# Attention's projections and the shares' transposition in the array's column halves, placed next to the values' product

## The chip, the cores and the metric

The kernel runs on one core of a Trainium2 chip. The time is the device time of one execution in microseconds (us); the kernel before took 5586.81 us (median of 3 runs, 5586.36 to 5594.37). Beside it stands one execution that the hardware profiler took, and all durations come from that one.

## The reference

The input is two images of 256 channels and 64x64 pixels, in fp32. Four layers follow each other:

```python
xn = group_norm(x)
q, k, v = split(einsum('bchw,oc->bohw', xn, w_qkv), 4 heads of 64 channels)
attn = softmax(einsum('bhci,bhcj->bhij', q, k) * 64 ** -0.5)
x = xn + einsum('bchw,oc->bohw', attn @ v, w_proj) + b_proj      # layer 0
x = x + position term                                            # layer 1
x = relu(x + bottleneck with one deformable 3x3 convolution)     # layer 2
x = x + two deformable 3x3 convolutions with group norms         # layer 3
```

The change is in layer 0: 4096 pixels attend to 4096 pixels, in 4 heads, for each of the two images.

## The kernel before, in words

The function `attention` (from L148 on) does layer 0 and, woven into it, much of layer 2; `deform` does what is left of layer 2 and layer 3 after it.

**Tiling of the attention.** A unit (`units`, L213) is one image and one pair of heads, so there are four. A unit has 256 steps (`per_unit`, L353). A step n takes 128 pixels of q, one head (h) and one of four chunks of 1024 keys (c), and a block is the 16 steps of 256 pixels of q. Each step runs through four functions:

- `scores` (L526) multiplies q by k (L533): contraction over the 64 channels of a head, so two products go side by side in the two row halves of the 128x128 array; the profile writes that as 64\*128 (64 rows by 128 columns). VectorE (DVE) takes the negated row maximum (`low`, L542).
- `exponentials` (L545) applies exp on ScalarE (ACT) with that maximum as bias (L549).
- `turn` (L555) transposes the exponentials with 16 matmuls of 64\*128 (L561) into two PSUM tiles `tt`; `keep` (L568) copies these to SBUF, one by ACT (L578) and the other by DVE (L576); from unit 2 on both go to ACT for h = 1.
- `attend` (L580) multiplies by the values (L588): contraction over 128 keys, 64 channels of output for each head, so two heads go side by side in the two column halves, written 128\*64.

All fp32 products but the transpositions stand in the profile as two matmul instructions each.

**Order of the work.** The engines run in the order in which the program is written (`manual_schedule`). The main loop takes two steps per turn. TensorE (PE) sees: the scores of steps n + 2 and n + 3; `small(n)`; `turn(n)`; the values' product of n - 4 and n - 3; `small(n + 1)`; `turn(n + 1)`; in units 2 and 3, a background step. On ACT the order is: copy of n - 1, `small(n)`, exp(n + 2), copy of n, `small(n + 1)`, exp(n + 3). On DVE: copy of n - 1, both maxima, `small(n)`, copy of n, the output of `attend`, `small(n + 1)`.

**What `small` runs.** `small(at)` (L635) runs what was registered for step `at` by `due` (L357), and where nothing was, in units 2 and 3, a background step of layer 2 (`background`, L606). Registered are:

- `make_q` (L243): the projection to q for the next 512 pixels, at even steps: 128\*128, two products of 512 columns (L247), then ACT scales it and a DMA turns the halves round. 31 of them stand in the main loop.
- `keys` (L257, matmuls L262), 24 of them: they use the column halves before the change already. One of two is at an odd step and one at an even one.
- `values` (L270, matmuls L275), 24: eight products of 128 columns, 128\*128; one of two at an odd step and one at an even one.
- For each block, `compare`, `raised`, `weights`, `spread`, `combine`: they turn the maxima and sums of the four chunks into shares. `spread` (L457), at an even step, transposes the 128x16 tile `share` (L460), DVE copies the result (L462), and DMAs write it to DRAM and read it back widened (`f`). `combine` multiplies the output of `attend` by it on POOL (L474 to L482), four steps later.
- For each pair of blocks, `project(0)` at an odd and `project(1)` at an even step (L493, matmul L498): 128\*128, one product of 512 columns each, then a DVE operation adds it to the residual `res`.
- In units 1 and 3, `second_layer` (L514) at an even step: layer 2's first product (L840, 128\*64) and its ACT operations.

All of these and the background steps write one PSUM tile, `pm`, which has one buffer (`pms`, L168); each waits until the one before it has been read by ACT or DVE.

Work in `begin` (L305), before the main loop, uses `make_q`, `keys` and `values` too.

Of the kernel before, what the change touches and what calls it, by code (L numbers as in the profile page):

```python
# [9 lines left out]
F32 = mybir.dt.float32  # L10
# [8 lines left out]
P = 128  # L19
# [19 lines left out]
class Net:  # L39
# [108 lines left out]
    def attention(self, bott):  # L148
# [4 lines left out]
        tc, nc, a = self.tc, self.nc, self.a  # L153
        with ExitStack() as ctx:
            wp = ctx.enter_context(tc.tile_pool(name="att_w", bufs=1))
            work = ctx.enter_context(tc.tile_pool(name="att_work", bufs=2))
            one = ctx.enter_context(tc.tile_pool(name="att_one", bufs=1))
# [18 lines left out]
            def ps(shape):  # L176
                return pms.tile(shape, F32, name="pm")

            def rows(t):
                return t.rearrange("(cb p) n -> p cb n", p=P)  # L180
# [8 lines left out]
            halves = [slice(0, 64), slice(64, 128)]  # L189
# [7 lines left out]
            for i in range(NB):  # L197
                t = xp.tile([P, 2, 512], F32, name="xb") if i < 4 else rest[:, i - 4]
                nc.sync.dma_start(t, rows(a["x"][0])[:, :, 512 * i : 512 * i + 512])
                first.append(t)  # L200
                if i == 1:
                    for j in range(2):
                        at = slice(64 * j, 64 * j + 5)
                        nc.sync.dma_start(wpos[at], a["wpos"])
                        nc.sync.dma_start(pos[at], a["pos"][:, :, P * j : P * j + P])
            wqkv = wp.tile([P, 2, 3 * C], F32, name="wqkv")
# [3 lines left out]
            wproj = wp.tile([P, 2, C], F32, name="wproj")  # L210
# [25 lines left out]
            def prepare(b):  # L236
                for coef in stats_of(b, (block(a["x"][b], i) for i in range(NB))):
                    yield True
                for i in range(NB):
                    normalize(b, i, coef, block(a["x"][b], i))  # L240
                    yield True

            def make_q(u, i, x, dst):  # L243

                hp = units[u][1]
                for cb in range(2):
                    nc.tensor.matmul(  # L247
                        dst, lhsT=wqkv[:, cb, hp * P : hp * P + P], rhs=x[:, cb, :],
                        start=(cb == 0), stop=(cb == 1),
                    )  # L250
                t, s = (qp.tile([P, 512], F32, name=n) for n in ("q", "qs"))
                nc.scalar.mul(t, dst, 64**-0.5)
                for j in range(2):
                    nc.sync.dma_start(s[halves[j], :], t[halves[1 - j], :])
                q[u, i] = (t, s)
# [14 lines left out]
            def values(u, x, dst):  # L270

                at = 2 * C + units[u][1] * P
                for n in range(4):
                    for cb in range(2):
                        nc.tensor.matmul(  # L275
                            dst[:, n * P : (n + 1) * P],
                            lhsT=x[:, cb, n * P : (n + 1) * P],
                            rhs=wqkv[:, cb, at : at + P],
                            start=(cb == 0),
                            stop=(cb == 1),  # L280
                        )

            def tiles(t):
                return t.rearrange("p (t c) -> p t c", c=P)
# [119 lines left out]
            class Block:  # L404
# [36 lines left out]
                def weights(self):  # L441

                    w = self.w
                    nc.vector.tensor_mul(self.sum, self.sum, w)
                    total = one.tile([P, 4], F32, name="total")
                    nc.vector.tensor_reduce(total, self.sum, AX.X, ALU.add)
                    nc.vector.reciprocal(total, total)
                    self.share = work.tile([P, 2, 4, 2], F32, name="share")
                    nc.vector.tensor_mul(
                        self.share.rearrange("p h c t -> p t h c"),  # L450
                        w.rearrange("p (t h) c -> p t h c", h=2),
                        total.rearrange("p (t h) -> p t h", h=2).unsqueeze(3).to_broadcast(
                            [P, 2, 2, 4]
                        ),
                    )

                def spread(self):  # L457

                    pt = ps([P, 512])[:16, :P]
                    nc.tensor.transpose(pt, self.share.rearrange("p h c t -> p (h c t)"), self.ident)  # L460
                    t = one.tile([16, P], F32, name="shares")
                    nc.vector.tensor_copy(t, pt)  # L462
                    d = self.share_d[self.i % 2]
                    nc.sync.dma_start(d, t)
                    self.f = one.tile([P, 4, 256], F32, name="f")
                    for h in range(2):
                        src = d[8 * h : 8 * h + 8].rearrange("(c t) q -> c (t q)", t=2)
                        nc.sync.dma_start(
                            self.f[halves[h]], src.unsqueeze(0).to_broadcast([64, 4, 256])
                        )  # L470
# [22 lines left out]
                def project(self, ob):  # L493
                    b, hp = units[self.u]
                    i = self.i // 2
                    oc = slice(ob * P, ob * P + P)
                    pp = ps([P, 512])
                    nc.tensor.matmul(  # L498
                        pp, lhsT=wproj[:, hp, oc], rhs=self.av, start=True, stop=True
                    )  # L500
                    res = self.res[:, ob, :]
                    if hp == 0:
                        nc.vector.scalar_tensor_tensor(
                            res, pp, self.vec[:, V_BPROJ + ob : V_BPROJ + ob + 1], res,
                            ALU.add, ALU.add,
                        )
                    else:
                        nc.vector.tensor_add(res, res, pp)
                    if ob == 1:
                        nc.sync.dma_start(  # L510
                            rows(self.xa_d[b])[:, :, 512 * i : 512 * i + 512], self.res
                        )
# [9 lines left out]
            def parts(n):  # L522
                u, r = divmod(n, per_unit)
                return u, r // 16, r % 16 // 4, r % 4 // 2, r % 2
# [43 lines left out]
            def keep(n, pts):  # L568
                u, i, c, t, h = parts(n)
                if n % 4 == 0:  # L570
                    ets[n // 4] = etp.tile([P, 8, 2, 256], F32, name="et")
                for j, pt in enumerate(pts):
                    at = P * t + 64 * j
                    dst = ets[n // 4][:, :, h, at : at + 64]
                    if j and (u < 2 or h == 0):
                        nc.vector.tensor_copy(dst, pt)  # L576
                    else:
                        nc.scalar.copy(dst, pt)  # L578
# [20 lines left out]
            def first_batch():  # L599
                yield from bott.conv(0, bt, ps)  # L600
                yield from self.early_image(bott, bt, ps)

            ets, now = {}, {}
            back = []

# [10 lines left out]


            pts, e = {}, {}
            ready = self.small.tile([P, 1], F32, name="ready")
            begin()  # L620
            n = 0
            while n < last + 4 or back or any(own.values()):
                u, d = divmod(n, per_unit)
                if d == 0 and u < len(units):
                    plan_unit(u)
                    if u == 0:
                        back.append(prepare(1))
                    if u == 1:
                        back.append(bott.before(0, bt, ps))
                    if u == 2:  # L630
                        back.append(first_batch())
                    if u == 3:
                        back.insert(0, bott.before(1, bt, ps))

                def small(at):  # L635
                    steps = own.pop(at, ())
                    for f in steps:
                        f()
                    if not steps and u > 1:
                        background(1)  # L640

                if n - 1 in pts:
                    keep(n - 1, pts.pop(n - 1))
                ahead = [(m, scores(m)) for m in (n + 2, n + 3) if m < last]
                small(n)
                for m in range(2):
                    if n < last:
                        pts[n + m] = turn(e.pop(n + m))
                    if ahead:
                        at, sc = ahead.pop(0)  # L650
                        e[at] = exponentials(at, sc)
                    if m == 0:
                        if n < last:
                            keep(n, pts.pop(n))
                        if 4 <= n < last + 4:
                            attend(n - 4)
                            attend(n - 3)
                        small(n + 1)
                if u or n % 8 == 0:
                    background(1)  # L660
                n += 2
# [813 lines left out]
```

## Time and profile before

| what | us |
|---|---|
| median of 3 runs | 5586.81 |
| the profiled execution's own time | 5402.33 |
| its span, first to last instruction | 5400.6 |
| from 0 to 75: start, positions, first q, k and v | 75 |
| from 75 to 1440: units 0 and 1, PE busy | 1351.92 of 1365 |
| from 1440 to 3140: units 2 and 3 with layer 2, PE busy | 1594.95 of 1700 |
| from 3140 to 5400: deformable convolutions, PE busy | 1972.77 of 2260 |

The time of an execution in the profiler is 3.3% under the median of the runs without it. A matmul's bar begins when the product starts to stream and is longer than the distance to the next one, since matmuls are pipelined: what a group costs PE is read from the start of its first matmul to the start of the next group's first. A group in the timeline (x16) is merged from so many instructions; the number after the start is its length. A name after the arrow in brackets says what ended an idle time.

### The profile page before, as it was taken

Reading aid. Unit: us, or ns where it says so; the run is one execution under the profiler, and the core shown is the slowest. Engines: PE = TensorE matmul, PEld = TensorE weight load, DVE = VectorE, ACT = ScalarE, POOL = GpSimd, SP = SyncE. Lnnn points to the kernel's source line nnn. Section 1 sums busy time; section 2 is a strip of 40 time slices with the busy share of each in tenths; the row PEclk is TensorE's granted clock in tenths of the full one; section 3 lists DMA queues with packets and bytes.
Section 4 is the critical chain, followed back from the end, with each engine's and each line's share of the span. In section 5 each row is a group of like instructions: output and inputs, shape, how many; then the busy total and the mean of one; then the engine's idle time right before and its main releaser. Section 6 shows DMA issues by size and latency. Waiting matters only on the chain.

```text
span 5400.6 us, 97530 instructions
## 1 busy us (share of the span) xinstructions
PE 4976.3 (92%) x37208; PEld 2665.3 (49%) x37208; DVE 4249.0 (79%) x8066; ACT 2897.7 (54%) x5333; POOL 2068.6 (38%) x1946
## 2 busy tenths in 40 slices
PE   8999999999999999999999977767899999999998
PEld 5555555555555555555555533333444444444443
DVE  6877767787668888677766648787899999999998
ACT  5676656666566666566666622222444444444444
POOL 0111101000024343233200047777566566656665
PEclk9999999999999999999999978888999999999999
DMA  5221111101113222222141146666999999999998
GB/s 168 62 89 58 41 64 39 48 29 44 48 54 89 77 82 90 80 78 74 50 136 34 35 156 231 225 223 231 353 333 330 341 360 358 352 390 353 342 349 320
DMA packets 347363, 920.29 MB, mean 170 GB/s; under 512 B 58972, under 2 KB 98698, under 8 KB 346894
## 3 DMA queue, kind: packets, MB, share of 16 engines
q0 software_dynamic: 193536, 679.59, 35.4%
q1 hardware_dynamic: 153358, 234.46, 13.5%
q8 instruction: 292, 4.78, 0.4%
q14 instruction: 177, 1.45, 0.1%
HBM read 815.90 MB, written 89.60 MB: 168 GB/s over the span
## 4 chain that ended last, share of the span: by engine, by line
PE 65%; DVE 17%; issue 6%; DMA 5%; ACT 5%; POOL 2%; SPq 0%; ACTq 0%; DVEq 0%; POOLq 0%
PE sc L533 14%; PE av L588 14%; PE out L1276 10%; PE tt L561 9%; DVE smp L1245 8%; PE pd L726 5%; DMA four<-img,didx 3%; PE pt L1257 3%; DVE low L542 2%; ACT e L549 2%; PE pm L976 1%; POOL bfour L766 1%; DVE bfour L947 1%; PE pm L498 1%; PE pm L247 1%
## 5 line engine op out<-in xcount | busy, mean ns | idle before, releaser
L1245 DVE SCALAR_TENSOR_TENSOR smp<-four,dw,smp 128x256 f32<-128x256 f32 x3456 | 1611.8, 483 | 168.5 <-ACT smp L1239 85.5
L549 ACT ACTIVATE e<-sc,low 128x1024 f32<-128x1024 f32 x1024 | 1147.5, 1121 | 646.0 <-DVE low L542 645.0
L542 DVE TENSOR_REDUCE low<-sc 128x1 f32<-128x1024 f32 x1024 | 1209.5, 1219 | 295.9 <-PE sc L533 288.2
L766 POOL DMA_INDIRECT four<-img,didx x1152 | 1161.5, 1008 | 656.8 <-DVE smp L1245 307.7
L1276 PE MATMUL out<-st,wc 128*128 128x512 f32 x2304 | 1236.8, 619 | 139.7 <-ACT st L1266 111.3
L533 PE MATMUL sc<-k,qs 64*128 64x512 f32 x2048 | 1029.0, 621 | 7.4 <-ACT e L549 7.1
L533 PE MATMUL sc<-k,q 64*128 64x512 f32 x2048 | 1018.7, 620 | 0.0
L588 PE MATMUL av<-et,v 128*64 128x256 f32 x8192 | 999.1, 386 | 0.0
L561 PEld LDWEIGHTS tt<-ident,e 64*128 64x128 f32 x16384 | 647.9, 140 | 559.1 <-issue 245.0
L474 POOL TENSOR_TENSOR o<-o,f 128x1024 f32<-128x1024 f32 x64 | 153.4, 2396 | 1967.1 <-DVE o L428 1182.8
L766 POOL DMA_INDIRECT bfour<-img,bidx x576 | 579.8, 1007 | 665.6 <-DVE bsmp L957 487.3
L561 PE MATMUL tt<-ident,e 64*128 64x64 f32 x16384 | 751.2, 228 | 86.5 <-ACT et L578 69.4
L578 ACT COPY et<-tt 128x512 f32<-128x512 f32 x1280 | 722.2, 587 | 83.7 <-PE tt L561 80.6
L1239 ACT ACTIVATE smp<-four,dw 128x256 f32<-128x256 f32 x1152 | 524.2, 503 | 430.6 <-DMA four<-img,didx 368.9
L576 DVE COPY et<-tt 128x512 f32<-128x512 f32 x768 | 524.6, 683 | 247.3 <-PE tt L561 245.8
L1257 PEld LDWEIGHTS pt<-ident,smp 128*128 128x128 f32 x2304 | 321.1, 144 | 740.7 <-issue 439.1
L1266 ACT COPY st<-pt 128x1024 f32<-128x1024 f32 x288 | 291.0, 1010 | 721.2 <-PE pt L1257 721.2
L588 PEld LDWEIGHTS av<-et,v 128*64 128x64 f32 x8192 | 544.8, 137 | 257.0 <-issue 1.3
L1276 PEld LDWEIGHTS out<-st,wc 128*128 128x128 f32 x2304 | 393.3, 197 | 402.2 <-issue 207.1
L1257 PE MATMUL pt<-ident,smp 128*128 128x128 f32 x2304 | 457.7, 281 | 67.0 <-DVE smp L1245 61.7
L726 PE MATMUL pd<-x,wf 128*126 128x512 f32 (+2 forms) x896 | 460.8, 601 | 8.4 <-DVE wf L1131 7.3
L533 PEld LDWEIGHTS sc<-k,qs 64*128 64x128 f32 x2048 | 351.2, 192 | 229.7 <-issue 123.6
(153 smaller groups left out, 3369.1 us busy)
## 6 DMA issues: line engine op xcount, KB each, us to landing
f<-share_d SPq DMA_DIRECT2D x128, 256.0 KB, 3.9
xb<-xn SPq DMA_DIRECT2D x55, 512.0 KB, 4.0
img<-imgt SPq DMA_DIRECT2D x96, 256.0 KB, 7.0
four<-img,didx POOLq DMA_INDIRECT x1152, 6.1
xa<-res SPq DMA_DIRECT2D x32, 512.0 KB, 2.7
xb<-in_x SPq DMA_DIRECT2D x20, 512.0 KB, 5.4
bfour<-img,bidx POOLq DMA_INDIRECT x576, 3.0
qs<-q SPq DMA_DIRECT2D x64, 128.0 KB, 4.0
```

The costliest lines, as they stand in the source:

```text
L533: nc.tensor.matmul(s[:, j, :], lhsT=q[u, i // 2][int(h != j)][halves[j], at : at + P], rhs=k[u][c][halves[j], h, :], start=True, stop=True,)
L542: nc.vector.tensor_reduce(low, s, AX.X, ALU.max, negate=True)
L549: nc.scalar.activation(e.rearrange("p j n -> p (j n)"), s, AF.Exp, bias=blk.low[:, g, c : c + 1], accum_out=blk.sum[:, g, c : c + 1],)
L561: nc.tensor.transpose(pt[:, m, :], e[half, m // 4, m % 4 * P : m % 4 * P + P], self.ident[half, half],)
L576: nc.vector.tensor_copy(dst, pt)
L578: nc.scalar.copy(dst, pt)
L588: nc.tensor.matmul(now["av"][halves[h], :], lhsT=v[u][c][:, m, halves[h]], rhs=ets[j][:, m, h, :], start=(m == 0), stop=(m == 7),)
L726: nc.tensor.matmul(pd[:m, r0 * W : r1 * W], lhsT=wt(s, t), rhs=src[:, (y + r0) * W : (y + r1) * W], start=(n == 0), stop=(n == len(srcs) * ...
L766: self.nc.gpsimd.indirect_dma_start(out=dst, out_offset=None, in_=img, in_offset=bass.IndirectOffsetOnAxis(ap=idx, axis=0),)
L1245: nc.vector.scalar_tensor_tensor(smps[s], four[:, c], weight(s, c), smps[s], ALU.mult, ALU.add)
L1257: nc.tensor.transpose(pts[u][:, c, j * P : (j + 1) * P], smp[:, c * P : c * P + P], self.ident,)
L1276: nc.tensor.matmul(outs[ob], lhsT=wc[k][:, c, ob * P : ob * P + P], rhs=sts[u][:, c, :], start=(k == 0 and c == 0), stop=(k == K2 - 1 and ...
```

## The change

Four edits inside `attention`:

1. `make_q`, `values` and `project` split each product into two with 64 columns of weights (pixels or output channels), which write partitions 0 to 63 and 64 to 127 of the same PSUM tile from the same moving operand. There are twice as many matmuls and weight loads, each with half of the columns.
2. `share` becomes one tile of 128x64, made and zeroed by POOL once before the main loop, in which `weights` fills the first 16 columns. `spread` transposes all 64, into 64 partitions, and copies 16 of these.
3. `small(n)` moves from between the scores and `turn(n)` to after `keep(n)`, right ahead of `attend(n - 4)`. PE then sees: scores, scores, `turn(n)`, `small(n)`, values' product, `small(n + 1)`, `turn(n + 1)`. On ACT `small(n)` comes after exp(n + 2) and the copy of n; on DVE after the copy of n. Background steps that run in `small(n)` move with it.
4. `ready`, a scratch column that is written once at the start, takes a buffer of another scratch tile.

```diff
@@ make_q
-                    nc.tensor.matmul(
-                        dst, lhsT=wqkv[:, cb, hp * P : hp * P + P], rhs=x[:, cb, :],
-                        start=(cb == 0), stop=(cb == 1),
-                    )
+                    for j in range(2):
+                        at = hp * P + 64 * j
+                        nc.tensor.matmul(
+                            dst[halves[j]], lhsT=wqkv[:, cb, at : at + 64], rhs=x[:, cb, :],
+                            start=(cb == 0), stop=(cb == 1),
+                        )
@@ values
-                        nc.tensor.matmul(
-                            dst[:, n * P : (n + 1) * P],
-                            lhsT=x[:, cb, n * P : (n + 1) * P],
...
+                        for j in range(2):
+                            px = n * P + 64 * j
+                            nc.tensor.matmul(
+                                dst[halves[j], n * P : (n + 1) * P],
+                                lhsT=x[:, cb, px : px + 64],
...
@@ weights
-                    self.share = work.tile([P, 2, 4, 2], F32, name="share")
                     nc.vector.tensor_mul(
-                        self.share.rearrange("p h c t -> p t h c"),
+                        share[:, :16].rearrange("p (h c t) -> p t h c", h=2, c=4),
@@ spread
-                    pt = ps([P, 512])[:16, :P]
-                    nc.tensor.transpose(pt, self.share.rearrange("p h c t -> p (h c t)"), self.ident)
+                    pt = ps([P, 512])[:64, :P]
+                    nc.tensor.transpose(pt, share, self.ident)
                     t = one.tile([16, P], F32, name="shares")
-                    nc.vector.tensor_copy(t, pt)
+                    nc.vector.tensor_copy(t, pt[:16])
@@ project
-                    nc.tensor.matmul(
-                        pp, lhsT=wproj[:, hp, oc], rhs=self.av, start=True, stop=True
-                    )
+                    for j in range(2):
+                        at = ob * P + 64 * j
+                        nc.tensor.matmul(
+                            pp[halves[j]], lhsT=wproj[:, hp, at : at + 64], rhs=self.av,
+                            start=True, stop=True,
+                        )
@@ attention, before and in the main loop
+            share = one.tile([P, 64], F32, name="share")
+            nc.gpsimd.memset(share, 0.0)
...
-            ready = self.small.tile([P, 1], F32, name="ready")
+            ready = self.small.tile([P, 4], F32, name="rs_t")[:, :1]
...
                 ahead = [(m, scores(m)) for m in (n + 2, n + 3) if m < last]
-                small(n)
                 for m in range(2):
                     if n < last:
                         pts[n + m] = turn(e.pop(n + m))
...
                     if m == 0:
                         if n < last:
                             keep(n, pts.pop(n))
+
+                        small(n)
                         if 4 <= n < last + 4:
                             attend(n - 4)
                             attend(n - 3)
```

More of the change, by code (lines that the diff above doesn't have):

```diff
@@ L274, in values @@
                     for cb in range(2):
-                        nc.tensor.matmul(
-                            dst[:, n * P : (n + 1) * P],
-                            lhsT=x[:, cb, n * P : (n + 1) * P],
-                            rhs=wqkv[:, cb, at : at + P],
-                            start=(cb == 0),
-                            stop=(cb == 1),
-                        )
+                        for j in range(2):
[3 more added lines that the diff above has]
+                                lhsT=x[:, cb, px : px + 64],
+                                rhs=wqkv[:, cb, at : at + P],
+                                start=(cb == 0),
+                                stop=(cb == 1),
+                            )
             def tiles(t):
@@ L495, in project @@
                     i = self.i // 2
-                    oc = slice(ob * P, ob * P + P)
                     pp = ps([P, 512])
-                    nc.tensor.matmul(
-                        pp, lhsT=wproj[:, hp, oc], rhs=self.av, start=True, stop=True
-                    )
+                    for j in range(2):
[3 more added lines that the diff above has]
+                            start=True, stop=True,
+                        )
                     res = self.res[:, ob, :]
```

## The prediction

> **What bounds the kernel now.** I read the busy time by stage first, to see where the edited code runs and which engine is full there.
>
> ```profile
> 75.00:1440.00 1365.00, 1351.92 (x14451) 779.07 (x14447) 1033.72 (x1499) 876.44 (x1621) 151.78 (x100) 1.00 0.17 52
> 1440.00:3140.00 1700.00, 1594.95 (x15697) 915.17 (x15697) 1219.08 (x1885) 1087.92 (x2022) 451.01 (x395) 0.97 0.24 72
> ```
>
> The columns are the stretch, its length, busy PE, weight loads, DVE, ACT and POOL (instructions in brackets), granted clock, DMA share and GB/s. All edited code runs in these two stretches and in the 75 us before them. In the first PE is busy 99%, in the second 94%; DVE has 76% and 72%, ACT 64% both times. PE sets the pace, alone in the first and nearly so in the second. After 3140 nothing is edited, so what attention saves should pass to the end as it is.
>
> Second, the waits of PE, for the second stretch: what it does when it isn't the bound.
>
> ```profile
> PE tt L561 <- ACT et L578: 60.7, 38, 3.4
> PE tt L561 <- DVE et L576: 14.9, 32, 1.6
> PE pm L904 <- ACT bod L895: 11.5, 7, 1.6
> ```
>
> (us in total, times, longest.) The first stretch has 5.3 us of the first kind and 1.0 of the second. So `turn` sometimes waits until `keep` has emptied its PSUM tile, and layer 2's background steps are what makes that late.
>
> Third, the timeline of PE, to price each step from start to start.
>
> ```profile
> 721.04 1.95 PE L588 MATMUL av<-et,v 128*64 128x256 f32 x16
> 722.82 1.89 PE L262 MATMUL pm<-xb,wqkv 128*64 128x512 f32 x8
> 724.63 0.71 PE L561 MATMUL tt<-ident,e 64*128 64x64 f32 x16
> ...
> 731.95 2.05 PE L275 MATMUL pm<-wqkv,xb 128*128 128x128 f32 x16
> 733.93 0.71 PE L561 MATMUL tt<-ident,e 64*128 64x64 f32 x16
> ...
> 776.81 0.66 PE L561 MATMUL tt<-ident,e 64*128 64x64 f32 x16
> 777.40 1.95 PE L588 MATMUL av<-et,v 128*64 128x256 f32 x16
> 779.28 0.71 PE L561 MATMUL tt<-ident,e 64*128 64x64 f32 x16
> 779.83 0.65 PE L533 MATMUL sc<-k,q 64*128 64x512 f32 x1
> ...
> 781.60 0.66 PE L561 MATMUL tt<-ident,e 64*128 64x64 f32 x16
> ...
> 788.86 1.13 PE L498 MATMUL pm<-avs,wproj 128*128 128x512 f32 x2
> 789.91 0.71 PE L561 MATMUL tt<-ident,e 64*128 64x64 f32 x16
> ...
> 801.25 0.65 PE L533 MATMUL sc<-k,q 64*128 64x512 f32 x1
> ...
> 803.11 0.28 PE L460 MATMUL pm<-ident,share 128*16 128x128 f32 x1
> 803.32 0.72 PE L561 MATMUL tt<-ident,e 64*128 64x64 f32 x16
> 803.97 1.95 PE L588 MATMUL av<-et,v 128*64 128x256 f32 x16
> ...
> 808.26 1.98 PE L247 MATMUL pm<-xb,wqkv 128*128 128x512 f32 x4
> 810.17 0.71 PE L561 MATMUL tt<-ident,e 64*128 64x64 f32 x16
> ```
>
> A plain turn of the loop is 4.79 us (776.81 to 781.60): transposes 0.59, values' product 1.88, transposes 0.55, scores 1.77. Watch the overlaps at the seams: the product with the values ends at 779.35 and the transposes start at 779.28, 0.07 earlier; where the form stays (64\*128 to 64\*128) the same seam overlaps by 0.16. The keys (L262) follow the product in its own form, and the two take 3.59 us together (721.04 to 724.63), only 1.71 more than the product alone. A seam between forms costs about 0.1 us.
>
> **What the Trainium skill says.** "TensorEngine Tiling (Array Packing)", Key Properties: "Changing tiling mode (not just tile) drains the TensorE". The trace agrees, at the 0.09 us above. Its Restrictions say that column tiling disables the transpose mode for fp32; but the shares' transposition is 128\*16 already and takes 277 ns, and layer 2's transposes take 297 ns as 128\*64 (L967) and 296 as 128\*128, so the trace shows no price. "TensorE: Matmul & The Clock Gate", Part 2, says that weight loads are pulled ahead of running matmuls and cost by columns; the trace has loads of 87 ns for 16 columns, 137 for 64 and 186 to 190 for 128, and no matmul waits for them. "PSUM — Partial Sum Buffer", on bank collisions, has it that different column tiles may write one bank at the same time; the keys do that in `pm` today.
>
> **The change part by part.** A step at an even place stands before between scores and transposes. It costs its own length, 0.09 for the seam after the scores and 0.06 for transposes that start cold: at 801.25 the scores take 1.86 to L460 instead of 1.77, and the transposes then take 0.65 instead of 0.59. So 0.15 plus its length. A step at an odd place follows the product and has one seam in its length. Afterwards both stand beside the product in its form, and cost their streaming alone: the keys' 1.71 for four pairs of 512 columns, 0.43 a pair. That halves run side by side is what the keys show; there each half has a moving operand of its own, in the new products both have the same.
>
> - `make_q`, 31 in the loop, even: 1.91 + 0.15 = 2.06 before; four pairs, 1.71 after. 31 x 0.35 = 10.9 us.
> - `project(1)`, even, 31: 1.05 + 0.15 = 1.20 before; two pairs, 0.86 after. 31 x 0.34 = 10.5 us.
> - `project(0)`, odd, 31: 1.05 against 0.86. 31 x 0.19 = 5.9 us.
> - Keys at even places, 12: 1.86 + 0.15 = 2.01 against 1.71. 3.6 us. The odd ones stay as they are.
> - Values: 16 instructions of 281 ns take 2.05, so one each (2.05 - 0.28) / 15 = 0.118. Sixteen pairs after: 1.89, if pairs keep that pitch. Twelve even ones, 1.98 + 0.15 = 2.13 before: 2.9 us; twelve odd ones, 1.98: 1.1 us. The unknown is the loads: 32 of 64 columns instead of 16 of 128. The product with the values has half of its 0.223 a pair as the lower bound, 0.11, or 1.8 us; if each load of 137 ns stood alone, 4.4 us, or 60 us lost over all 24. I take 0.118, since the transposes load 128 columns into each of two halves every 0.07 us.
> - Shares, 63 beside scores: 0.21 + 0.15 = 0.36 before; one product of 128 columns, 0.12 after. The load of 64 columns instead of 16 is hidden as others are. 63 x 0.24 = 15.1 us. The memset and the 48 zero columns cost PE nothing, and DVE the same copy of 16 rows.
> - Layer 2's first product (L840), 15 even: 1.86 + 0.15 against 1.71. 4.5 us. Background steps in `small(n)`: 13 groups of full-array transposes lose one of two seams, 0.15 each, and two groups of 128\*64 0.3: 2.6 us.
> - `begin` (a few seams) and `ready`: under 1 us, not counted.
>
> Sum: 10.9 + 10.5 + 5.9 + 3.6 + 2.9 + 1.1 + 15.1 + 4.5 + 2.6 = **57 us**, half of it in each stretch.
>
> **What the move delays.** On ACT the step's copy now stands ahead of exp(n + 3) and no longer ahead of exp(n + 2). For `make_q`: from the start of the scores, PE ends q at 1.77 + 0.59 + 1.71 = 4.1; ACT copies until 4.9, exp ends at 6.1. The scores that need that PSUM tile start at 4.1 + 1.88 + 0.55 + 0.86 = 7.4: 1.3 us of cover. The single buffer of `pm` is now read while only the product (1.88) runs, before transposes too: ACT's 4.9 or DVE's copy after `keep` at about 4.8 against 6.0 for the odd step. Where keys and shares fall on one step (3 times), PE waits about 0.8 as it does today. Odd values and keys still delay exp, and the scores after them wait 0.5 as now. The shares' DMAs (SP) and `f` come about 0.7 us later, after `keep`'s copy on DVE; POOL's `combine` waits for them or for the output of `attend`, and is done over 3 us before DVE writes that buffer again; its gathers behind it lose at most those 0.7. In the second stretch DVE's copy in `keep` no longer stands behind `small(n)`, which takes from the 14.9 us; but two background steps now stand ahead of exp(n + 3), which can give it back. I count it at nothing, between 15 gained and 15 lost.
>
> The profiled execution would go from 5402.33 to 5345, 1.1% less. The median is 184 us above it, for reasons that the profile doesn't show; I subtract the same 57 there: 5587 - 57 = **5530 us**.
>
> **The rivals.**
> - *Second half absorbed.* If units 2 and 3 follow the chain scores, maximum, exp, `keep` and not PE, only the first stretch's half counts: 28 us, 5558. For it: that chain leaves under 0.1 us in a plain turn there (ACT's copy starts at 1501.71 and takes 0.58, and the transposes start at 1502.40). Against: the steps lie in turns that are longer on PE.
> - *The halves don't run side by side when they share the moving operand.* Then q costs 1.71 more, a projection 0.86, values 1.89: 31 x 1.71 + 62 x 0.86 + 24 x 1.89 = 152 us, less 57: 95 slower, 5682. It decides from 38% lost overlap on. Against: keys and the values' product overlap fully, with other operands.
> - *Waits shrink too*, by more than 15 us: 5510.
>
> **How the numbers follow.** Main case 5530 (5512 to 5546): 0.66. Half absorbed, 5546 to 5575: 0.17. More gained, 5500 to 5512: 0.07. About no change: 0.04. Slower: 0.06. Range 5508 to 5562. Faster 0.9, within 0.2% 0.04, slower 0.06; 0.2%, 11 us, is about what a measurement of this kernel can tell.
>
> **What would show it.** q as eight instructions of 128\*64 in about 1.8 us, projections as four in about 1.0, values as 32 in about 2.0, each right before or after the values' product; scores 1.77 to the transposes in nearly all turns; PE's waits in the second stretch within 15 us of before. Bars twice as long for q would show serial halves; more waits of `tt` for `et` absorption.

## The result, and the profile after

| kernel | median us | lowest to highest | runs |
|---|---|---|---|
| before | 5586.59 | 5586.31 to 5594.37 | 4 |
| after | 5527.18 | 5524.51 to 5538.85 | 4 |

The ratio is 0.9885 (95% interval 0.9866 to 0.9904): 59 us less, where 57 had been forecast. The span of the profiled execution of after is 5527.0 us (5528.8 with what lies around it), near its median.

That span can't be set against the 5400.6 us of the profile shown for before: the runs below show that chips differ. One takes about 5407 us for the kernel before, others 5587 to 5594, two 5648 to 5649 (medians), and the first profile has the length of the short kind. Which chip gave it isn't on record, so it is inferred, not shown, that its distance of 184 us from the median is this difference. Hence both kernels were run once more on one chip (e8 is before, e9 is after; line numbers in after are 2 to 9 higher). The busy time by stage, e8 first; the stretches are cut where ACT starts exp number 0, number 512 and number 1023 in each, so they are units 0 and 1, units 2 and 3, and what follows. Columns: stretch, length, busy PE, weight loads, DVE, ACT, POOL, granted clock, DMA share, GB/s.

```profile
60.50:1490.30 1429.80, 1411.17 (x14989) 815.23 (x14991) 1068.24 (x1550) 907.21 (x1680) 153.57 (x101) 1.00 0.18 55
1490.30:3157.70 1667.40, 1544.81 (x15160) 881.73 (x15160) 1194.55 (x1835) 1061.92 (x1972) 448.19 (x392) 0.97 0.25 71
3157.70:5650.40 2492.70, 2014.61 (x6825) 947.18 (x6821) 1965.58 (x4631) 892.16 (x1655) 1453.28 (x1445) 0.91 0.81 284
```

The same view of after (e9):

```profile
59.50:1461.90 1402.40, 1381.48 (x15361) 819.72 (x15361) 1063.88 (x1551) 908.24 (x1678) 153.59 (x101) 1.00 0.19 56
1461.90:3092.80 1630.90, 1510.20 (x15458) 890.44 (x15454) 1181.55 (x1836) 1061.86 (x1973) 449.95 (x392) 0.97 0.26 73
3092.80:5589.10 2496.30, 2018.80 (x6829) 947.73 (x6825) 1965.64 (x4631) 891.88 (x1655) 1451.24 (x1445) 0.91 0.81 284
```

Units 0 and 1 lost 27.4 us, units 2 and 3 lost 36.5, the start lost 1.0, and what follows took 3.6 more: together 61.3. In the first two stretches the length falls by about what PE's busy time falls (29.7 and 34.6), and PE stays busy 99% and 93% of them. So the gain is PE's, and it reached the end.

How a step now stands, in PE's timeline of after, start to start. The shares and the values first:

```profile
186.70 0.30 PE L463 MATMUL pm<-ident,share 128*64 128x128 f32 x1
186.93 1.95 PE L593 MATMUL av<-et,v 128*64 128x256 f32 x16
188.81 0.71 PE L566 MATMUL tt<-ident,e 64*128 64x64 f32 x16
...
702.71 1.90 PE L593 MATMUL av<-et,v 128*64 128x256 f32 x16
704.44 1.92 PE L279 MATMUL pm<-wqkv,xb 128*64 128x128 f32 x32
706.29 0.71 PE L566 MATMUL tt<-ident,e 64*128 64x64 f32 x16
```

The shares take 0.23 (186.70 to 186.93) and not 0.12: their bar overlaps the product after them by 0.07, which is the overlap of a seam, though both stand as 128\*64. The values and the product take 3.58 (702.71 to 706.29), which leaves 1.70 for the values beside the 1.88 of a product alone, where the forecast had 1.89. Their 16 pairs follow each other at 0.109, 1.75 in all, instead of 0.118.

What each step is worth is best read over whole turns of the loop, from the start of one turn's scores to the start of the next's. Worked out from the two traces of e8 and e9, for units 0 and 1:

| what the turn holds beside its four plain groups | turns | before, mean us | after, mean us | difference | forecast |
|---|---|---|---|---|---|
| nothing | 157 | 4.822 | 4.818 | 0.00 | 0 |
| `project` | 30 | 5.962 | 5.688 | -0.27 | -0.34 even, -0.19 odd |
| shares | 22 | 5.147 | 5.016 | -0.13 | -0.24 |
| q | 11 | 6.855 | 6.594 | -0.26 (medians: -0.35) | -0.35 |
| keys and values | 11 | 9.179 | 8.712 | -0.47 | -0.39 or -0.24 |
| layer 2's first product, transposes of `h` | 6 | 7.483 | 6.628 | -0.86 | -0.30 |
| q, layer 2's L892 and L913 | 5 | 9.236 | 9.629 | +0.39 | -0.35 |

The last two rows are the surprises, and both are waits. The first of them before (e8), all engines, around L840:

```profile
965.86 1.36 ACT L850 ACTIVATE h<-pm,bn_t,bn_s 64x512 f32<-64x512 f32 x3 [3.05 <-PE pm L840]
...
967.22 1.10 ACT L549 ACTIVATE e<-sc,low 128x1024 f32<-128x1024 f32 x1
...
968.28 0.27 PE L561 MATMUL tt<-ident,e 64*128 64x64 f32 x1
968.31 0.57 ACT L578 COPY et<-tt 128x512 f32<-128x512 f32 x1
...
968.94 0.71 PE L561 MATMUL tt<-ident,e 64*128 64x64 f32 x15 [0.39 <-ACT et L578]
```

Then after, in an earlier such turn:

```profile
867.13 1.50 PE L849 MATMUL pm<-res,w 128*64 128x512 f32 x3
...
868.33 0.58 ACT L583 COPY et<-tt 128x512 f32<-128x512 f32 x1
...
869.11 1.07 ACT L859 ACTIVATE h<-pm,bn_t,bn_s 64x512 f32<-64x512 f32 x2 [0.20 <-PE pm L849]
...
870.72 0.71 PE L566 MATMUL tt<-ident,e 64*128 64x64 f32 x16
```

Before, the step's activations (L850) run on ACT ahead of exp, and the copy of n comes behind both at 968.31; the other 15 transposes of the second step wait for it and start 0.66 after the first. After, the copy (868.33) comes before the activations (869.11), and nothing waits. L849 and the values' product still take 3.59 together (867.13 to 870.72), just as keys and product do: 1.71 for the step, as forecast.

The other row, after, around the q of such a turn, all engines:

```profile
1049.00 2.05 ACT L904 ACTIVATE bod<-pm,boff 32x504 f32<-32x504 f32 x3 [2.29 <-PE pm L892]
...
1051.06 0.59 ACT L583 COPY et<-tt 128x512 f32<-128x512 f32 x1
...
1051.70 0.71 PE L566 MATMUL tt<-ident,e 64*128 64x64 f32 x15 [0.97 <-ACT et L583]
...
1052.34 1.94 PE L249 MATMUL pm<-xb,wqkv 128*64 128x512 f32 x8
...
1054.11 1.90 PE L593 MATMUL av<-et,v 128*64 128x256 f32 x16
...
1055.93 0.71 PE L566 MATMUL tt<-ident,e 64*128 64x64 f32 x16
```

Layer 2's activations (L904) of the step before keep ACT until 1051.06, and the copy that frees `tt` is late. Before, q stood between the scores and these transposes and took 2.06 us, so that the copy was done; now the transposes come first and wait 0.97. The projection itself costs what was forecast: q and the product take 3.59 together (1052.34 to 1055.93), 1.71 for q.

The same wait, shorter, stands in two of the 11 turns with q alone, both in unit 0, and it makes their mean fall less than their median. They take 7.01 instead of 6.50. There ACT is busy with the normalization of the second image (L229) ahead of the copy, all engines of after:

```profile
274.96 1.51 ACT L229 ACTIVATE xb<-xb,gn_sh,gn_sc 128x512 f32<-128x512 f32 x2
...
276.36 0.58 ACT L583 COPY et<-tt 128x512 f32<-128x512 f32 x1
...
277.00 0.71 PE L566 MATMUL tt<-ident,e 64*128 64x64 f32 x16 [0.29 <-ACT et L583]
```

What PE waits for in units 2 and 3; before (e8), then after (e9):

```profile
PE tt L561 <- ACT et L578: 72.2, 50, 3.6
PE tt L561 <- DVE et L576: 15.8, 29, 1.6
```

```profile
PE tt L566 <- ACT et L583: 76.9, 52, 4.0
...
PE tt L566 <- DVE et L581: 1.9, 2, 1.3
```

The waits for DVE's copy are gone, as argued, since that copy no longer stands behind `small(n)`. ACT's grew by 4.7, and those with no releaser that the trace shows ("issue") grew from 6.8 to 9.3. Of 94.8 us in all three 88.1 are left.

### The profile page after: what moved, and what is told of

The parts are those of the page before. It is cut to its first block, busy times and chain, and to the rows that moved or that the text cites. A ratio compares the mean times of both kernels' runs of the same rounds, so it can differ in the third digit from the quotient of the medians.

```text
span 5527.0 us, 99087 instructions
## 1 busy us (share of the span) xinstructions
PE 4928.5 (89%) x37976; PEld 2677.3 (48%) x37976; DVE 4232.0 (77%) x8066; ACT 2888.5 (52%) x5333; POOL 2069.2 (37%) x1947
## 4 chain that ended last, share of the span: by engine, by line
PE 64%; DVE 16%; issue 8%; ACT 6%; another core or an unknown queue 4%; DMA 1%; POOL 1%; ACTq 0%; SPq 0%; DVEq 0%; POOLq 0%
PE av L593 14%; PE sc L538 14%; PE out L1285 10%; PE tt L566 9%; DVE smp L1254 8%; PE pd L735 5%; PE pt L1266 3%; DVE low L547 2%; ACT e L554 2%; DVE bfour L956 1%; PE pm L985 1%; DVE bfour L965 1%; PE pm L502 1%; PE pm L249 1%
## 5 line engine op out<-in xcount | busy, mean ns | idle before, releaser
L538 PE MATMUL sc<-k,qs 64*128 64x512 f32 x2048 | 1026.4, 620 | 10.1 <-ACT e L554 9.5
L566 PEld LDWEIGHTS tt<-ident,e 64*128 64x128 f32 x16384 | 662.8, 139 | 582.1 <-issue 287.1
L566 PE MATMUL tt<-ident,e 64*128 64x64 f32 x16384 | 731.2, 227 | 96.0 <-ACT et L583 80.3
L593 PEld LDWEIGHTS av<-et,v 128*64 128x64 f32 x8192 | 558.3, 137 | 306.7 <-issue 57.8
L735 PE MATMUL pd<-x,wf 128*126 128x512 f32 (+2 forms) x896 | 463.0, 604 | 10.1 <-issue 9.2
```

The source lines that it names most:

```text
L538: nc.tensor.matmul(s[:, j, :], lhsT=q[u, i // 2][int(h != j)][halves[j], at : at + P], rhs=k[u][c][halves[j], h, :], start=True, stop=True,)
L566: nc.tensor.transpose(pt[:, m, :], e[half, m // 4, m % 4 * P : m % 4 * P + P], self.ident[half, half],)
L593: nc.tensor.matmul(now["av"][halves[h], :], lhsT=v[u][c][:, m, halves[h]], rhs=ets[j][:, m, h, :], start=(m == 0), stop=(m == 7),)
L735: nc.tensor.matmul(pd[:m, r0 * W : r1 * W], lhsT=wt(s, t), rhs=src[:, (y + r0) * W : (y + r1) * W], start=(n == 0), stop=(n == len(srcs) * ...
```

## The experiments

The runs of e0 to e3 share one chip and its runs of the kernel before (median 5407.05 us), e4 to e7 another (5648.15), e8 to e10 a third (5649.28), and e11 has a fourth (5594.18). Each chip was used for one batch of runs, so a difference between chips can't be told from one between batches. Ratios are to those runs, with 95% intervals. "Attention" is the time from the first exp to exp number 1023, in the one profiled execution of each run. In units 0 and 1 it agrees within 0.2 us between executions of one kernel, on all chips, so these are compared across chips too; units 2 and 3 are not that steady.

### e0: the kernel before, once more

No edit.

> The kernel before, profiled once more, because its first profiled execution took 5402 us where its timed runs take 5587. Theory 1 (the deformable part after attention varies with the execution, attention doesn't): if it takes about 5587 us, attention ends at 3149 +- 5 us as in the first profile and the stretch after it is 165 to 185 us longer. Theory 2 (attention itself was favoured in the first profile): attention ends at 3165 us or later.

0.9998 (0.9989 to 1.0007), 5404.35 us. The execution was a short one, so neither theory, both about a long one, was tested. Attention took 3071.6 us (1429.8 in units 0 and 1, 1641.8 in units 2 and 3), the first profile's 3065.7 (1429.9 and 1635.8). So the first profile is reproduced, and here the runs without the profiler are as short as it: the profiler doesn't shorten an execution, and the distance to 5587 isn't its doing.

### e1: the move alone

```diff
@@ before, main loop
-                small(n)
...
                         keep(n, pts.pop(n))
+                        small(n)
```

> The kernel before with small(n) moved next to the values' product, and no product split. Theory 1 (seams): every product that stood between scores and transposes saves 0.15 us (149 of them, 22 us), and layer 2's first product (15) and the keys at even places (12) now stand beside the values' product in its form (17 and 2 us): 41 us less on PE, of which the first stretch keeps nearly all and the second loses half to waits: 25 to 35 us, ratio 0.994 to 0.9955. Theory 2 (the move brings nothing, all comes from the halves): within 5 us of before.

0.9886 (0.9872 to 0.9901), 62 us, more than theory 1 gave. Units 0 and 1 lost 14.2 against e0, units 2 and 3 lost 56.1. By turns, in units 0 and 1: shares 5.15 to 5.00, q 6.85 to 6.70, layer 2's first product 7.53 to 6.63 (medians), which the forms have no part in. The shares' transposition is still 128\*16 here and takes 0.21 beside the product, less than the 0.23 of after:

```profile
799.01 0.28 PE L460 MATMUL pm<-ident,share 128*16 128x128 f32 x1
799.22 1.95 PE L588 MATMUL av<-et,v 128*64 128x256 f32 x16
```

So the place brought all that the shares gained, and the 64 columns brought nothing. The large gain in units 2 and 3 didn't come back on another chip (e10).

### e2: the halves alone

```diff
@@ after, main loop
+                small(n)
...
                         keep(n, pts.pop(n))
-                        small(n)
```

> The kernel after with small(n) back between scores and transposes. Theory 1 (seams): only the steps at odd places, which stand beside the values' product anyway, gain: 31 projections 0.2 us, 12 values 0.24 us; the others gain 0.05 to 0.13 us each by a better pitch: 10 to 15 us less, ratio 0.997 to 0.998. Theory 2 (halves stream faster wherever they stand): most of the 59 us.

0.9975 (0.9964 to 0.9986), 11 us, as theory 1 had it. Units 0 and 1 lost 7.3 us against e0. At the old place a q turn falls only by 0.05, to 6.81, where it falls to 6.50 in after: the narrow form frees no seam there, since the scores before it and the transposes after it have another form. For q the move alone is worth 0.15, the halves alone 0.05, and both together 0.35. The turn with shares gets 0.02 longer (5.17), so the 64 columns don't help at this place either.

### e3: the background steps left at the old place

```diff
@@ after, main loop
+                early = n if n not in own else None
+                if early is not None and u > 1:
+                    background(1)
...
-                    if not steps and u > 1:
+                    if not steps and u > 1 and at != early:
```

> The kernel after, but a background step of layer 2 that runs at step n stays between scores and transposes; only the registered steps move. Theory 1 (in units 2 and 3 two background steps now stand together ahead of exp(n + 3), and the waits of the transposes for the copies eat the gain): units 2 and 3 get 8 to 20 us shorter than with the change. Theory 2 (the waits come from the copy of n - 1, which the moved registered step no longer covers, or from background work wherever it stands): within 5 us of the kernel after.

0.9901 (0.9886 to 0.9916), 54 us; units 0 and 1 as in after (1402.6), units 2 and 3 38.7 less than e0. PE's waits for DVE's copy in units 2 and 3 stay at 15.6 (15.0 in e0), so it is the background steps, not the registered ones, that held that copy up. After itself didn't run on this chip, so no difference to it is left to read: inconclusive on the time, clear on the wait.

### e4: the kernel after, on another chip

No edit.

> The kernel after once more, beside the kernel before and with a profile, since its first profile fell to an execution of the longer kind (deformable part 2416 us), and that of before to one of the shorter kind (2251 us). Theory 1 (seams and halves, and fewer waits in units 2 and 3 from the moved background steps): units 0 and 1 end 28 us earlier as in the first profile, units 2 and 3 gain 50 us as with the move alone: 72 to 86 us less where before takes 5407, ratio 0.984 to 0.987. Theory 2 (the first profile of after tells all: units 2 and 3 gain 10 us): 38 us less, ratio 0.993.

0.9902 (0.9881 to 0.9924), 56 us: between the two expectations, and what the first comparison gave. Units 0 and 1 took 1402.3.

### e5: the shares as a product

```diff
@@ after, spread
-                    nc.tensor.transpose(pt, share, self.ident)
+                    nc.tensor.matmul(pt, lhsT=share, rhs=self.ident, start=True, stop=True)
```

> The kernel after, with the shares multiplied by the identity as an ordinary product instead of transposed. Theory 1 (between a transposition and a product there is a seam although both are 128*64; that is why the shares' step costs 0.23 us and not 0.12): the step is two instructions with no seam to the values' product, and costs 0.1 to 0.2 us: 2 to 8 us less than the kernel after. Theory 2 (the 0.23 us is the load or the single half): two instructions cost more than one, 5 to 10 us more than the kernel after.

0.9909 (0.9887 to 0.9931): no gain over e4. The step and the product together take 2.09 us, 2.11 in after, and a turn with shares 5.00 instead of 5.01:

```profile
186.27 0.32 PE L463 MATMUL pm<-ident,share 128*64 128x128 f32 x1
186.28 0.43 PE L593 MATMUL av<-et,v 128*64 128x256 f32 x1
186.43 0.27 PE L463 MATMUL pm<-ident,share 128*64 128x128 f32 x1
186.54 1.89 PE L593 MATMUL av<-et,v 128*64 128x256 f32 x15
```

There are two passes now. The values' product starts beside the first, and the bar of the second overlaps it by 0.16, so the seam is gone; but the two passes cost 0.21 over the 1.88 of the product alone, about what the one with its seam did. The seam of theory 1 is seen, its gain isn't.

### e6: layer 2's first product moved alone

```diff
@@ before, plan
-                            due(at + 30, self.second_layer)
+                            late.setdefault(at + 30, []).append(self.second_layer)
@@ before, main loop
...
-                    if not steps and u > 1:
+                    if not steps and u > 1 and at not in late:
                         background(1)
...
                             keep(n, pts.pop(n))
+                        for f in late.pop(n, ()):
+                            f()
```

> The kernel before, with layer 2's first product (second_layer, 15 in the loop) moved next to the values' product, and nothing else. Theory 1 (it fills one column half alone, and the values' product of the other half starts beside it): 0.86 us instead of 2.01 each, 1.15 x 15 = 17 us less, ratio 0.9968. Theory 2 (what the prediction said, seams alone): 4.4 us less, ratio 0.9992.

Attention fell by 15.5 us against e8, which ran on another chip: 5.4 in units 0 and 1, and 10.1 in the others, where the chip may have a share. By turns it fell from 7.53 to 6.63, as in after. That is theory 1's size, but its reason doesn't hold: L842 and the product together take 3.59 (1138.93 to 1142.52), so the step costs 1.71. The 0.86 that the expectation gives counts the product from the third of its matmuls, which leaves out 0.85. What is saved is the wait of 0.6 that is shown above for e8, and 0.3 that remains for the seams. By the timed runs the ratio is 0.9993 (0.9978 to 1.0008): the gain in attention is not seen in the whole.

### e7: the background steps moved alone

```diff
@@ before, main loop; small(n) returns True where a background step is due
                     if not steps and u > 1:
+                        if at == n:
+                            return True
                         background(1)
...
-                small(n)
+                later = small(n)
...
                         keep(n, pts.pop(n))
+                        if later:
+                            background(1)
```

> The kernel before, with only the background steps of layer 2 that run at step n moved next to the values' product. Theory 1 (DVE's copy in keep no longer stands behind a background step, so the transposes' 15 us of waits for it go, and some of those for ACT's): units 0 and 1 unchanged, units 2 and 3 15 to 30 us shorter, ratio 0.9945 to 0.997. Theory 2 (the waits only change their place): within 5 us of before.

0.9994 (0.9977 to 1.0011). The waits of PE in units 2 and 3:

```profile
PE tt L561 <- ACT et L578: 77.4, 54, 3.8
PE tt L561 <- issue: 13.4, 8, 3.1
```

For DVE's copy it waits 1.8 instead of 15.8 in e8 (on another chip that takes about as long), for ACT's 77.4 instead of 72.2, and "issue" has doubled from 6.8. By the time that is theory 2, no gain. Of the 14 us that DVE's waits lost 12 are back with the others: the waits change place. For this part the forecast's "nothing" is right, on this chip.

### e8 and e9: both kernels on one chip

No edit.

> The kernel before, profiled on the same chip as the next two: the chips differ (before takes 5407 us on one, 5587 and 5648 on others), and so far no chip has given a profile of before and of after. Theory 1 (the longer chips are longer in units 2 and 3 too, where layer 2's gathers run, by some 40 us): on a long chip attention ends at 3155 to 3175 us. Theory 2 (they are longer after attention only): at 3130 to 3150 us. Units 0 and 1 end at 1490 us either way.

> The kernel after on the chip of the two others. Theory 1 (the halves add to the move in units 0 and 1, 14 us, and nothing in units 2 and 3, where waits take it): units 0 and 1 end 28 us before those of before, units 2 and 3 gain 25 to 50 us, in all 55 to 75 us. Theory 2 (the halves gain in units 2 and 3 as well): 80 us or more, 25 us under the move alone.

e8: 1.0003 (0.9988 to 1.0019). Units 0 and 1 take what they take everywhere (1429.8); units 2 and 3 take 1667.4, 26 and 32 more than in e0 and in the first profile, and what follows takes 2492.7 where the first profile has 2274.2. So chips differ in both, as theory 1 had it; for units 2 and 3 that rests on one execution each.

e9: 0.9884 (0.9863 to 0.9905), 57 us by the medians and 61 by the spans, within theory 1's 55 to 75, and units 2 and 3 within its 25 to 50 (36.5).

### e10: the move alone, on this chip

The edit is that of e1.

> The move alone, on the chip of the two others. Theory 1: 10 to 20 us longer than the kernel after, by what units 0 and 1 lose without the halves. Theory 2: 25 us or more longer. Theory 3 (the move was favoured by its chip, and the halves carry the change elsewhere): units 2 and 3 gain under 20 us.

0.9911 (0.9887 to 0.9934), 42 us by the medians, 15 more than e9's time, which is theory 1's size; the lengths of single runs overlap (5577 to 5605 in e9, 5589 to 5625 here). In the trace attention took 3063.5, 30.2 more than e9's 3033.3: 13.2 in units 0 and 1, and 17.0 in units 2 and 3. The first shows that the halves gain. The second is no more than what that stretch varies by between executions of after (16 us), but PE's busy time in it is 16.8 longer too (1527.0 against 1510.2). So theory 1's reason, that waits take there what the halves give, gets no support, and theory 2's point, that they gain in both, is likely and not shown.

The move's gain in units 2 and 3 is 19.5 here and was 56.1 on the first chip. By the medians the two gains are 42 and 62 us, with intervals that overlap (37 to 64 and 54 to 69). PE's waits for both copies fell there by 21 us (75.7 in e0, 54.8 in e1) and here by 11 (88.0 to 76.6). Its busy time fell there by 41.4 and here by 17.9.

### e11: q left at its old place

```diff
@@ after, plan
...
-                    due(
-                        n0 + 32 * i - 14,
-                        lambda i=i: make_q(u, i, x.pop(("q", i))[0], ps([P, 512])),
-                    )
+                    first_q[n0 + 32 * i - 14] = (
+                        lambda i=i: make_q(u, i, x.pop(("q", i))[0], ps([P, 512]))
+                    )
+                    due(n0 + 32 * i - 14, lambda: None)
@@ after, main loop, before turn(n)
+                if n in first_q:
+                    first_q.pop(n)()
```

> The kernel after, but 28 of the 31 projections to q (still in halves) stay between scores and transposes. Units 0 and 1 are read from the trace, where executions of one kernel agree within 1 us. Theory 1 (in unit 1 the moved projection no longer covers the copy of n - 1, which ACT does only after layer 2's 2 us of shifts; the transposes wait 1.2 us at each such turn): unit 0 gets 2 to 3 us longer than with the change (7 seams of 0.3), unit 1 gets 1 to 5 us shorter, since five to seven waits of 1.2 us go. Theory 2 (no such cover): units 0 and 1 each get 2 to 3 us longer.

0.9893 (0.9864 to 0.9922). Unit 0, where layer 2 isn't woven in, takes 684.8 us instead of 683.7. Two or three more had been expected from seven turns at 0.31 each; but for the two of them that wait behind L229 in after the old place is 0.2 shorter, which makes the sum 1.1. Unit 1, where layer 2 is woven in, takes 717.0 instead of 718.7. PE's waits in unit 1, in after and then in e11:

```profile
PE tt L566 <- ACT et L583: 5.8, 6, 1.0
```

```profile
PE pm L249 <- ACT bod L906: 2.1, 5, 0.4
...
PE tt L566 <- ACT et L583: 1.0, 1, 1.0
```

Five waits of nearly 1.0 us are gone, and five of 0.4 for `pm` are there instead. So it is the place of q that made the last row of the table: as cover it was worth more there than the seams that its move frees (these five turns take 8.66 instead of 9.10, apart from the 0.53 of L892 ahead of the scores). It is a matter of 2 us, which the trace of units 0 and 1 can tell and the times can't.

## Why the prediction was right

**The bound.** "PE sets the pace, alone in the first and nearly so in the second": right. PE's busy time fell by 29.7 and 34.6 us in the two stretches and their lengths by 27.4 and 36.5; 57 were forecast, half in each. **The end**: "what attention saves should pass to the end as it is": right within 4 us (2492.7 and 2496.3).

**Seams and halves.** The q turns fell by 0.35 (median) and the projections by 0.27 on average, where 0.35 and 0.265 were forecast: halves that share a moving operand run side by side, so the rival that they don't is excluded. Keys and product are as before.

**Shares**: 0.13 instead of 0.24. The step that failed is "one product of 128 columns, 0.12 after": it costs 0.23. It rests on the reading that "the trace shows no price" for a transposition in the column form. The length of the instruction shows none, but its seams do. Two places of the trace before show it:

```profile
1703.95 1.95 PE L588 MATMUL av<-et,v 128*64 128x256 f32 x16
1705.83 0.41 PE L967 MATMUL pm<-ident,bsmp 128*64 128x128 f32 x2
...
3804.25 0.38 PE L1257 MATMUL pt<-ident,smp 128*128 128x128 f32 x2
3804.47 0.60 PE L967 MATMUL pm<-ident,bsmp 128*64 128x128 f32 x4
3804.90 1.02 PE L1276 MATMUL out<-st,wc 128*128 128x512 f32 x2
```

The product of 128\*64 overlaps the transposes of 128\*64 that follow it by 0.07 (a seam), and takes 1.88 up to them, where it takes 1.78 up to the keys. In the second place transposes of the same form, 128\*64, stand between work of 128\*128 and overlap it by 0.16 to 0.17 on both sides (no seam). It is so in all 14 traces, one place of 187 beside full-array work apart: at its seams such a transposition behaves like work of the full array. In the row form there is no such thing, since the transposes of 64\*128 and the scores overlap by 0.16. So the shares' step still has a seam on either side, and its 0.13 came from its place alone (e1). The missing 0.11 on 63 steps is 7 us.

**Values**: pairs take 0.109, not 0.118, and turns with keys and values gained 0.47 where 0.24 or 0.39 were forecast; 3 to 4 us more over 24 steps. The 0.118 was a mean: in the trace before the first two of the 16 instructions start 0.213 apart and the others 0.112.

**Layer 2's first product**: 0.86 to 0.90 instead of 0.30, 8 to 9 us more over 15 steps. The 0.30 of seams is there; the wait of 0.6 that its activations had caused was in the trace and wasn't priced.

**The cover of q**: the prediction found 1.3 us of cover for what follows q and didn't ask what q itself had covered. The late copy costs 0.74 a turn against the forecast (+0.39 for -0.35), five times in unit 1, and 0.51 twice in unit 0, nearly 5 us in all.

**Waits in units 2 and 3.** "Between 15 gained and 15 lost": the three kinds fell by 6.7. The 15 of DVE went as argued, and half came back with ACT and "issue". So nothing was absorbed there, and the rival *Second half absorbed* (28 us in all) falls. In the traces units 2 and 3 lost 36.5, more than their half. Between executions that stretch varies by 16 us (after: 1625.3, 1641.4 and 1630.9), so the medians are the better witness: 59, 56 and 57 us were gained in three comparisons (the first one, e4 and e9), and the least that their intervals allow is 43 us.

The total of 57 came out because the terms erred both ways: 7 too much for the shares and nearly 5 for q's cover, against 8 to 9 too little for layer 2's product and 3 to 4 for the values. That they cancel to within 1 us is luck; the bound and the seams were right. That the median lies 184 us above the profile "for reasons that the profile doesn't show" was, as far as can be inferred, a difference of chips, and taking the same 57 off it was right: 57 to 61 on the third chip, 59 in the first comparison.

**Open.** Why the move alone gains 36.6 us more in units 2 and 3 on one chip than on another isn't settled. Of these 23.5 are PE's busy time, in a stretch where the granted clock was 0.97 in e0 and 0.98 in e1, but 0.97 in both e8 and e10; 13.1 are PE's idle time. So the clock may have favoured e1, and with one execution each that can't be shown. Nor is it settled why those units and what follows them run longer on some chips, while units 0 and 1 of the kernel before agree within 0.2 us.

## What to carry to other kernels

Price a small step of PE over a whole turn of the loop, from one fixed group to the next: the seams on its two sides, its streaming, and what its successors wait for. Here a step that changed the array's form paid for two seams, and making it narrow helped only where it then stood beside work of the same form (q: 0.05 by the form, 0.15 by the place, 0.35 by both). Whether a step has really taken on a form is read from its overlaps with its neighbours, and not from its label or its length: the shares' transposition was labelled 128\*64 and kept its seams. Before a step is moved, ask of both its places which buffer it gives time to come free there, and which other engine's queue its own follow-up work stands in.

## What was not expected of the hardware

- Two neighbours with the label 128\*64 can still have a seam: an fp32 transposition and a product overlap by 0.07 us, where product and product overlap by 0.17. The same transposition overlaps work of 128\*128 by 0.16. The shares' step costs 0.23 as 128\*64, 0.21 as 128\*16 (e1), and 0.21 as two passes of a product without a seam (e5).
- Chips differ by more than the change is worth: 5407, 5587 to 5594 and 5648 to 5649 us for the kernel before. The part in which PE alone sets the pace (1429.8 us) is the same wherever it was profiled. What differs has PE below its full clock (0.97 and 0.91 in e8, 0.97 and 0.94 in the first profile) and, in the last part, a lower DMA rate (284 GB/s in e8, 312 in the first profile); which of these is the cause, if either, isn't shown.
